# Expert tiles of two 64-row units, each with an expert of its own, in place of 128-row tiles of one expert

## The chip, the core and the metric

The kernel runs on one core of a Trainium2 chip. The metric is the device time of one execution in microseconds (us). The core has a matrix engine (TensorE: PE in the profile, its weight loads PEld), a vector engine (VectorE, DVE), a scalar engine (ScalarE, ACT), a general engine (GpSimd, POOL) and a queue engine for transfers (SyncE, SP). Each takes its instructions in order. They run beside each other and wait for each other through semaphores. Matrix products land in PSUM, eight banks of it; everything else stands in SBUF or in device memory.

## What is computed

The input is 8 sequences of 256 rows with 128 features, 2048 rows in all, in fp32. Six layers follow each other. Two of them, the first and the third, are a mixture of experts; between them stands a causal attention of 16 heads with 8 features each, and after them come a gated mixer, a layer of nine gated shifts, and the mixer again.

```python
x = x + 0.5 * moe(layernorm(x))      # L0_ffn
x = x + attention(layernorm(x))      # L0_attn
x = x + 0.5 * moe(layernorm(x))      # L0_ffn
x = x + 0.5 * mixer(layernorm(x))    # L1_ffn
x = x + shifts(layernorm(x))         # L1_attn
x = x + 0.5 * mixer(layernorm(x))    # L1_ffn
```

The layer that the change is about, cut to its core. Each row goes to 2 of 8 experts, so there are 4096 pairs of a row and an expert:

```python
normed = rmsnorm(x, norm_weight)
probs = softmax(normed @ router_weight.T)
topk_w, topk_idx = top_k(probs, 2); topk_w = topk_w / sum(topk_w)
for e in range(8):
    gate, up = split(normed @ gate_up_weight[e].T)    # 352 columns each
    out_e = (silu(gate) * up) @ down_weight[e].T      # 352 to 128
    moe_out += combine[:, e] * out_e
return x + alpha * moe_out
```

## The kernel before

**A planner writes the order.** No loop issues instructions directly. The kernel records operations with their engine, an estimated duration, what they need, and the buffers that they take and free (`Work`, `Op`, `Buf`). `Work.issue` then goes through the ready operations, takes the one that can start first by its own estimates (nearly equal starts go to the one with the longest way to the end), and emits it. This fixes the order on every engine. Constants called `BIAS` move whole groups of operations ahead or back in that ranking. When the planner foresees an idle matrix engine, it fills the time with matmuls of no use (`pw`), which keep that engine's clock up. All instructions pass one helper, so nearly every row of the profile bears its line, L65; rows are told apart by their tiles. The row of value loads bears L74.

**Groups.** The rows stand in four groups of 512 (`NG`, `GT`), each of four 128-row blocks.

**The expert layer.** `moe_route` norms a group, writes it to device memory (`rows0`, `rows1`), multiplies by the router weights and finds the two best experts of each row. `moe_plan` runs twice in a layer: after the first two groups (`whole` false), and after all four. It counts rows by expert and gives each pair a slot such that every 128-row tile holds one expert. Then it inverts this: `hits` marks which tile a pair is in, `is_at` marks which row of the tile it has, times the row's number, and `find` multiplies both on the matrix engine, which gives for every tile the list of rows to gather (`take`). `which_expert` and `side_by_side` give each tile its expert (`expert`). `ASIDE` names the blocks of `is_at` that ScalarE makes; VectorE makes the rest.

Since an expert's last tile may be part empty, `TILES` is 39 for 32 full tiles, 9 of which come from the first plan. `moe_experts` gathers the rows of a tile (`xs`, one indirect transfer by GpSimd), transposes them (`pt`) and scales them by the norm weight (`nT`). `moe_tile` does the rest: a value load brings the tile's expert number into a register of the matrix engine (`number`), which then addresses the weights (`gu`, `dw`, resident in SBUF); two products of 352 columns (`pg`, `pu`); SiLU on ScalarE (`sg`); the product with `pu` on VectorE (`hid`); three transposes (`ph`), a copy out of PSUM on ScalarE (`hT`), three accumulating products (`po`), a copy on VectorE (`ys`), and a store to device memory by SP. Beginning a tile waits for tiles two and three behind it, so that about three tiles are under way at once. `moe_back` scales the group's own rows on ScalarE (`own_rows`), gathers both results of each row (`back`), and adds them with their weights.

**Attention.** Scores (`sc`) run on strips of 32 rows of the matrix array, weighted values (`po<-ep,va`) on strips of 32 columns, four strips at once. Masks, transposes and projections use the full array. The last tiles of the first expert layer run among the first groups' attention, and the second expert layer starts where the attention ends.

Of the kernel before, what the change touches and what calls it, by code (L numbers as in the profile page):

```python
# [19 lines left out]
P = 128  # L20
NG = 4
GT = 4
# [8 lines left out]
TILES = 2 * NT + 7  # L31
# [4 lines left out]
BIAS = (10.0, 28.0, 18.0, 0.0, 19.0, 22.0, -6.0)  # L36
# [14 lines left out]
ASIDE = ((1,), (2, 5))  # L51
FOLD = ((4, 4, 1), (2, 2, 2, 2, 1), (4, 4, 1), (4, 2, 1, 1, 1))


class InOrder:
# [16 lines left out]
    def value_load(self, *args, **kw):  # L72
        with self.tc.issue_after(self.last.ins):
            return self.engine.value_load(*args, **kw)  # L74

# [18 lines left out]
class Op:  # L94
    def __init__(self, engine, us, do, needs, takes, uses, lag, spare):
        self.engine, self.us, self.do, self.lag, self.spare = engine, us, do, lag, spare
        self.takes, self.uses = takes, uses
        self.needs = [n for n in needs if n is not None]
        self.out, self.end, self.rank, self.back = None, None, None, 0.0


class Work:
# [25 lines left out]

    def __getattr__(self, name):
        if name not in ("pe", "dve", "act", "pool", "sp"):  # L130
            raise AttributeError(name)
        return lambda us, do, *needs, **kw: self.op(name, us, do, needs, **kw)

    def start(self, op):
        t = self.free.get(op.engine, 0.0)
# [84 lines left out]
def tile_macaron(ctx: ExitStack, tc: tile.TileContext, a: dict, out: bass.AP):  # L220
# [64 lines left out]
    with nc.allow_low_precision("zeros and ones"):  # L285
# [25 lines left out]
    minus_tok = ctile("minus_tok", [P, NT])  # L311
    nc.vector.tensor_scalar(minus_tok, tok1, -1.0, None, ALU.mult)
# [16 lines left out]
    va = [ctile(f"va{k}", [P, GT, NH, 32]) for k in range(2)]  # L329
# [9 lines left out]
            "t": 11, "q": 10, "p": 4, "mix": 2, "yTs": 2, "yTg": 2, "vT": 2,  # L339
# [15 lines left out]
    w.idle = idle  # L355

# [100 lines left out]

    def moe_layer(n, first):

        few = 2 * GT * first - 7  # L460
# [6 lines left out]
        for name, shape, dtype in (  # L467
            ("top", [P, NT, 8], F32), ("which", [P, NT, 8], U32), ("w", [P, NT, 2], F32),
            ("ab", [P, 2, NT], F32), ("rs", [P, NT], F32), ("slot", [P, 2 * NT], U32),
            ("take0", [P, few], U32), ("take1", [P, TILES - few], U32), ("expert", [1, TILES], I32),  # L470
# [12 lines left out]
    def moe_route(g, r):  # L483
# [33 lines left out]
        def scale_rows():  # L517
            nT = wtile(tag, "nT", (P, GT * P))
            nc.scalar.activation(
                nT, pt.out.rearrange("p t d -> p (t d)"), AF.Copy, scale=norm_w  # L520
            )
            return nT

        nT = w.act(0.69, scale_rows, pt, fewer, uses=[b1], takes=[nTb])
# [83 lines left out]
    def moe_plan(r, whole):  # L608
# [10 lines left out]
        def small(name, shape, dtype=F32):  # L619
# [4 lines left out]
                oh=2 * NT * E, m=NT * E, slot=NT * E, past=3 * NT * E, sums=P, hit=wide,  # L624
# [70 lines left out]
        def ends():  # L695

            whole = small("whole", [P, E])
            nc.vector.tensor_scalar(whole, placed.out[:, nt, :], -63.5, 1.0 / P, ALU.add, ALU.mult)
            nc.vector.tensor_scalar(whole, whole, ROUND, ROUND, ALU.add, ALU.subtract)
            nc.vector.tensor_tensor_scan(r["end"], one8, whole, 0.0, ALU.mult, ALU.add)  # L700
            nc.vector.tensor_scalar(r["full"][:, 0, :], whole, float(P), None, ALU.mult)
            nc.vector.scalar_tensor_tensor(
                r["base"], r["end"], float(P), r["full"][:, 0, :], ALU.mult, ALU.subtract
# [14 lines left out]
        def all_ends():  # L718
# [9 lines left out]
            nc.vector.tensor_scalar(left, left, 63.5, 1.0 / P, ALU.add, ALU.mult)  # L728
# [3 lines left out]
            if soon:  # L732
# [4 lines left out]
                    full[:, 2, :], nr[:, 1, :], float(P), full[:, 1, :], ALU.mult, ALU.add  # L737
# [5 lines left out]
            for k in range(parts):  # L743
# [9 lines left out]
                up[:, 0, :], at2[:, 0, :], float(P), r["both"], ALU.mult, ALU.subtract  # L753
            )
            nc.vector.tensor_tensor(up[:, 1:, :], at2[:, 1:, :], at2[:, :-1, :], ALU.subtract)
            nc.vector.tensor_scalar(up[:, 1, :], up[:, 1, :], -1.0, float(P), ALU.add, ALU.mult)
            if soon:
                nc.vector.tensor_tensor(up[:, 2, :], up[:, 2, :], nr[:, 1, :], ALU.subtract)
                nc.vector.tensor_scalar(up[:, 2, :], up[:, 2, :], float(P), None, ALU.mult)
# [13 lines left out]
        def prepare():  # L773
            full = r["full"]
            nc.vector.tensor_scalar(full[:, 1, :], full[:, 0, :], float(P), None, ALU.add)
# [38 lines left out]

        def find(k, at):
            if k == 0:
                v["pi"] = bank([P, ns], "pi")
            for j in range(GT):
                i = GT * k + j
                nc.tensor.matmul(  # L820
                    v["pi"], lhsT=at.out[:, j, :], rhs=v["hit"][:, i, :], start=(i == 0),
# [3 lines left out]
        def is_at(k):  # L825
            tag = "ata" if k in by_act else "at"
            at = wtile(tag, tag, (P, GT, P), F16)
            for j in range(GT):
                i = GT * k + j
                token = tok1[:, i % nt : i % nt + 1]  # L830
                if k in by_act:
# [4 lines left out]
                    nc.scalar.activation(  # L836
                        at[:, j, :], at[:, j, :], AF.Relu, bias=token,
                        scale=minus_tok[:, i % nt : i % nt + 1],
                    )
                else:  # L840
                    nc.vector.tensor_scalar(
                        at[:, j, :], iota_r, v["row"][:, i : i + 1], token, ALU.is_equal, ALU.mult
                    )
            return at

        found = None
        for k in range(2 * nt // GT):
            ab = Buf("ata" if k in by_act else "at")
            at = (w.act if k in by_act else w.dve)(
                2.0 if k in by_act else 0.68, lambda k=k: is_at(k), rowed, takes=[ab]  # L850
            )
            found = w.pe(
                0.3, lambda k=k, at=at: find(k, at), at, hit, found,
# [9 lines left out]
        def which_expert():  # L863
# [6 lines left out]
                le, until.rearrange("p k e -> p (k e)"), float(-n0), tok1[:, 0:1], ALU.add,  # L870
# [12 lines left out]
        def side_by_side():  # L883
            pe = bank([1, ns], "pe")
            nc.tensor.matmul(
                pe, lhsT=v["ef"][0:ns, :], rhs=ident[0:ns, 0:ns], start=True, stop=True
# [5 lines left out]
            0.17, lambda: nc.vector.tensor_copy(r["expert"][:, n0:n1], aside.out), aside,  # L892
# [9 lines left out]
    def moe_experts(r, sizes):  # L902
# [4 lines left out]
        for h in range(2):  # L907
            plan = r["plan"][h]
            rows = r["all_stored" if h else "stored"].values()
            for n in sizes[h]:  # L910
# [28 lines left out]
                def scale_rows(n=n, pt=pt):  # L939
                    nT = wtile("nT", "nT", (P, GT * P))  # L940
                    nc.scalar.activation(
                        nT[:, : n * P], pt.out.rearrange("p t d -> p (t d)")[:, : n * P], AF.Copy,
                        scale=norm_w,
# [3 lines left out]
                nT = w.act(0.2 + 0.125 * n, scale_rows, pt, uses=[b1], takes=[nb])  # L947
# [10 lines left out]
    def moe_tile(r, plan, k, nT, nb, j, pus, turned, downs, numbers):  # L958
# [3 lines left out]
        def number():  # L962
            numbers[k] = nc.tensor.value_load(
                r["expert"][0:1, k : k + 1], min_val=0, max_val=E - 1
            )

        known = w.pe(0.03, number, plan["experts"], *pus[-2:-1], lag=0.8)

        def product(c):
            wt = gu[:, bass.ds(numbers[k], 1), :].rearrange("p o h -> p (o h)")  # L970
            out = bank([P, HID], "pg" if c == 0 else "pu")
            nc.tensor.matmul(
                out, lhsT=nT.out[:, bass.ts(j, P)], rhs=wt[:, HID * c : HID * (c + 1)],
                start=True, stop=True,
            )
            return out

        pg = w.pe(0.6, lambda: product(0), known, nT, weights, *pus[-1:], *turned[-2:-1], *downs[-3:-2],
                  takes=[bg], uses=[nb], spare=3)
        pu = w.pe(0.6, lambda: product(1), pg, takes=[bu], uses=[nb])  # L980
# [34 lines left out]
        def keep():  # L1015
            hT = wtile("hT", "hT", (P, len(HC), P))
            nc.scalar.copy(hT, ph.out)
            return hT

        hT = w.act(0.48, keep, ph, takes=[tb], uses=[bh])  # L1020

        def down():
            po = bank([P, P], "po")
            wt = dw[:, bass.ds(numbers[k], 1), :, :].rearrange("p o c d -> p (o c) d")
            for c in range(len(HC)):
                nc.tensor.matmul(
                    po, lhsT=hT.out[:, c, :], rhs=wt[:, c, :], start=(c == 0),
                    stop=(c == len(HC) - 1),
                )
            return po  # L1030

        po = w.pe(0.67, down, hT, takes=[bo], uses=[tb])
        downs.append(po)

        def result():
            ys = wtile("ys", "ys", (P, P))
            nc.vector.tensor_copy(ys, po.out)
            return ys

        ys = w.dve(0.29, result, po, takes=[yb], uses=[bo])  # L1040
# [6 lines left out]
    def moe_back(g, r, stored):  # L1047
# [4 lines left out]
        if g < r["first"]:  # L1052
            until = 2 * GT * r["first"] + E
        elif r["soon"] and g < r["soon"]:
            until = 2 * GT * r["soon"] + E

        def own_rows():
            for t in range(GT):
                i = GT * g + t
                nc.scalar.activation(  # L1060
                    x[g][:, t, :], x[g][:, t, :], AF.Identity,
                    bias=r["ab"][:, 1, i : i + 1], scale=r["ab"][:, 0, i : i + 1],
                )

        changes(g, w.act(1.7, own_rows, hold["affined"], *tokens[g].given, *tokens[g].read))
# [37 lines left out]
    def attention():  # L1103
# [6 lines left out]
        def constants(mask, step):  # L1110
# [20 lines left out]
        va_free = [  # L1131
            [w.pool(1.4, lambda v=v: nc.gpsimd.memset(v[:, :, :, DK:32], 1.0))] for v in va
        ]
# [8 lines left out]
        def enter(g):  # L1142
# [6 lines left out]
            def keep(tag, name, src):  # L1149
                dst = wtile(tag, name, (P, GT * P))  # L1150
                nc.scalar.copy(dst, src)
                return dst

            yT = w.act(
                0.6, lambda: keep("nT", "yT", pt.out.rearrange("p t d -> p (t d)")), pt,
# [9 lines left out]
            cT = w.act(0.6, lambda: keep("cT", "cT", pc.out), pc, takes=[cb], uses=[b2])  # L1165
# [5 lines left out]
            for h2 in range(2):  # L1171
# [23 lines left out]
                def put(k, h2=h2, pj=pj):  # L1195
                    hg = 2 * h2 + k // 2
                    if k % 2 == 0:
                        nc.scalar.copy(box["qT"][:, hg, :], pj.out[k])
                    elif k == 1:
# [8 lines left out]
                for k in range(4):  # L1208
                    entered.append((w.dve if k == 1 else w.act)(
                        0.69 if k % 2 else 0.6, lambda k=k, f=put: f(k), pj, ones,  # L1210
# [4 lines left out]
            def value_rows():  # L1215
                pv = bank([P, GT * P], "pv")
                for t in range(GT):
# [7 lines left out]
            values = w.dve(  # L1225
                0.69,
                lambda: nc.vector.tensor_copy(
                    va[g % 2][:, :, :, 0:DK],
# [134 lines left out]
    def weighted(i, q, s, group, va_free):  # L1363

        g, t0 = i // 2, 2 * (i % 2)
        vb, ab, tb = Buf("b"), Buf("av"), Buf("b")

        def values():
            po = bank([P, 4, P], "po")
            for hg in range(4):  # L1370
                for k in range(q + 1):
                    for j in range(4):
                        nc.tensor.matmul(
                            po[32 * j : 32 * j + 32, hg, :],
                            lhsT=va[g % 2][:, t0 + k, 4 * hg + j, :],
# [11 lines left out]
        def keep():  # L1387
            av = wtile("av", "av", (P, 4, P))
            nc.scalar.copy(av, po.out)
            return av  # L1390

        av = w.act(0.6, keep, po, takes=[ab], uses=[vb])
# [26 lines left out]
        def keep_o():  # L1419
            oT = wtile("oT", "oT", (P, 2, P))  # L1420
            nc.scalar.copy(oT, pt.out[:, 0:2, :])
            return oT

        oT = w.act(0.4, keep_o, pt, takes=[ob], uses=[b1])
# [16 lines left out]
    def mix(g, n):  # L1441
# [8 lines left out]
        def keep():  # L1450
            yT = stile("yTs", "yTs", (P, 2, S + 1))
            nc.scalar.activation(yT[:, :, 0:1], one8[:, 0:2].unsqueeze(2), AF.Copy, scale=0.0)
            nc.scalar.copy(yT[:, :, 1 : S + 1], pt.out.rearrange("p (b t) d -> p b (t d)", b=2))
# [328 lines left out]
```

## Time and profile before

| | us |
|---|---|
| median of 3 runs | 516.03 |
| lowest and highest of them | 515.32, 517.52 |
| the profiled execution | 516.23 |
| its span, first to last instruction | 514.2 |

The profile lists the busy time of each engine, slices of the span, the chain of work that ended last (followed back from the end), and groups of instructions with their mean duration, shapes and what they waited for. A matmul in fp32 shows as two records, its two passes; a transpose shows as one. Matmuls overlap, so that a row's mean duration says less than the distance between two starts.

```profile
PE   7778889999999999999999999899999999999995
DVE  7866323436776897577768268634336537989960
ACT  3416537644436546546547563547645476666542
PEclk9989889999999999999999999799999999999998
```

These are 40 slices of 12.9 us each; a digit is the busy share in tenths, PEclk the granted clock in tenths. The expert layers lie in slices 3 to 12 and 24 to 32.

```profile
L65 PE MATMUL pg<-gu,nT 128*128 x156 | 62.4, 483 | 4.0 <-issue 1.9 <-ACT nT L65 1.6 <-DMA rows<-ep 0.5
L65 PE MATMUL po<-ep,va 128*32 128x128 f32 x768 | 24.3, 275 | 0.0
L65 ACT COPY hT<-ph 128x384 f32<-128x384 f32 x78 | 37.1, 478 | 55.5 <-PE ph L65 52.5 <-PE pu L65 2.4 <-PE po L65 0.4
L65 ACT ACTIVATE sg<-pg 128x352 f32<-128x352 f32 x78 | 36.2, 464 | 36.4 <-PE pg L65 34.7
L65 DVE TENSOR_TENSOR hid<-sg,pu 128x352 f32<-128x352 f32 x78 | 40.6, 521 | 68.7 <-PE pu L65 53.4 <-ACT sg L65 11.0 <-ACT nT L65 2.6
L65 DVE COPY ys<-po 128x128 f32<-128x128 f32 x78 | 22.2, 289 | 25.4 <-PE po L65 21.5 <-PE pt L65 1.6
```

A group's row reads: line, engine, operation, tile written and tiles read, the part of the matrix array (rows*columns), shapes, how often; then busy time in us and mean ns of one; then the engine's idle time just before, and what ended it.

### The profile page before, as it was taken

To read this page: it belongs to the slowest core of one execution; us is meant where nothing else is said; L and a number is where in the kernel's file an instruction comes from. 1 tells how busy PE (TensorE), PEld (TensorE's weight loads), DVE (VectorE), ACT (ScalarE), POOL (GpSimd) and SP (SyncE) were. 2 spreads that over 40 slices of the span, in tenths; PEclk is the share of its full clock that TensorE was granted. 3 is DMA by queue.
4 is the path that set the end of the run, shared out by engine and by line. 5 is a ranking of instruction groups with operands and counts; after the bars stand their busy time and mean duration, and the time that the engine had idled before them with its cause. 6 is when DMAs were issued, how large, how long until landed. Compare 5 with 4: busy or idle time off the path is not lost.

```text
span 514.2 us, 12524 instructions
## 1 busy us (share of the span) xinstructions
PE 485.9 (94%) x4594; PEld 344.7 (67%) x4594; DVE 321.1 (62%) x1119; ACT 272.5 (53%) x584; POOL 225.4 (44%) x237
## 2 busy tenths in 40 slices
PE   7778889999999999999999999899999999999995
PEld 3435767877676666777777776577887875575673
DVE  7866323436776897577768268634336537989960
ACT  3416537644436546546547563547645476666542
POOL 8060578456203720000000340478657758867631
PEclk9989889999999999999999999799999999999998
DMA  8850122223101100000100020122332210000001
GB/s 270 262 164 23 49 71 57 61 62 70 27 17 33 54 18 3 23 3 3 64 3 3 23 68 11 41 84 57 71 67 72 66 38 20 2 1 1 22 20 41
DMA packets 27034, 26.24 MB, mean 51 GB/s; under 512 B 4064, under 2 KB 24288, under 8 KB 26560
## 3 DMA queue, kind: packets, MB, share of 16 engines
q1 hardware_dynamic: 21232, 15.60, 9.9%
q0 software_dynamic: 4544, 9.32, 7.5%
q8 instruction: 38, 0.62, 0.5%
q10 hardware_dynamic: 1200, 0.53, 0.4%
q14 instruction: 20, 0.16, 0.1%
HBM read 17.18 MB, written 9.31 MB: 51 GB/s over the span
## 4 chain that ended last, share of the span: by engine, by line
PE 69%; DVE 13%; POOL 5%; issue 4%; DMA 4%; ACT 4%; POOLq 0%; SPq 0%; DVEq 0%; ACTq 0%
PE sc L65 17%; PE po L65 15%; PE pg L65 8%; PE pu L65 8%; PE ph L65 5%; PE pt L65 4%; DVE x L65 3%; PE pgt L65 2%; POOL back L65 2%; PE pr L65 2%; DMA rest<-in_rest 2%; DMA rows<-n 2%; DVE p L65 2%; PE pv L65 2%; PE pj L65 1%
## 5 line engine op out<-in xcount | busy, mean ns | idle before, releaser
L65 POOL DMA_INDIRECT xs<-rows,take x78 | 74.6, 956 | 120.8 <-DVE take L65 42.8
L65 POOL DMA_INDIRECT back<-ys,slot x64 | 61.4, 959 | 61.5 <-DMA ys<-ys 33.7
L65 DVE TENSOR_TENSOR hid<-sg,pu 128x352 f32<-128x352 f32 x78 | 40.6, 521 | 68.7 <-PE pu L65 53.4
L65 ACT ACTIVATE ep<-sc 128x512 f32<-128x512 f32 x96 | 52.0, 595 | 52.6 <-PE sc L65 52.6
L65 PEld LDWEIGHTS po<-dw,hT 128*128 128x128 f32 x468 | 62.8, 192 | 15.4 <-ACT hT L65 2.0
L65 PE MATMUL po<-dw,hT 128*128 x468 | 65.5, 277 | 1.2 <-ACT hT L65 0.4
L65 ACT COPY hT<-ph 128x384 f32<-128x384 f32 x78 | 37.1, 478 | 55.5 <-PE ph L65 52.5
L65 PE MATMUL pg<-gu,nT 128*128 x156 | 62.4, 483 | 4.0 <-issue 1.9
L65 POOL TENSOR_TENSOR stats<-stats,minus_half 128x4 f32<-128x4 f32 x28 | 28.7, 1025 | 82.5 <-DVE stats L65 81.9
L65 PE MATMUL pu<-gu,nT 128*128 x156 | 60.6, 470 | 0.0
L65 PEld LDWEIGHTS sc<-kT,qT 32*128 32x128 f32 x768 | 46.0, 186 | 19.6 <-issue 16.8
L65 PE MATMUL sc<-qT,kT 32*128 32x128 f32 x768 | 56.2, 283 | 0.7 <-DVE qT L65 0.5
L65 ACT ACTIVATE sg<-pg 128x352 f32<-128x352 f32 x78 | 36.2, 464 | 36.4 <-PE pg L65 34.7
L65 PE MATMUL sc<-kT,qT 32*128 32x128 f32 x768 | 55.1, 283 | 0.0
L65 DVE TENSOR_REDUCE mtmp<-sc 128x4 f32<-128x512 f32 x64 | 41.3, 684 | 15.5 <-PE sc L65 15.5
L65 PEld LDWEIGHTS sc<-qT,kT 32*128 32x128 f32 x768 | 46.9, 186 | 3.3 <-issue 2.1
L65 PE MATMUL ph<-ident,hid 128*128 128x128 f32 x234 | 39.6, 282 | 1.8 <-DVE hid L65 1.7
L65 PEld LDWEIGHTS ph<-ident,hid 128*128 128x128 f32 x234 | 30.3, 146 | 16.3 <-issue 8.3
L65 PE MATMUL pw<-before,ones_b 128*128 128x512 bf16 x125 | 36.0, 426 | 3.3 <-POOL ones_b L65 2.4
L65 DVE COPY ys<-po 128x128 f32<-128x128 f32 x78 | 22.2, 289 | 25.4 <-PE po L65 21.5
L65 PE MATMUL pgt<-yTg,rest 128*128 128x512 f32 x72 | 34.2, 595 | 0.7 <-DVE p L65 0.7
L65 PEld LDWEIGHTS pu<-gu,nT 128*128 128x128 f32 x156 | 27.2, 198 | 7.7 <-issue 1.0
(204 smaller groups left out, 885.7 us busy)
## 6 DMA issues: line engine op xcount, KB each, us to landing
ys<-ys SPq DMA_DIRECT2D x78, 64.0 KB, 2.0
gu<-in_guT SPq DMA_DIRECT2D x2, 1408.0 KB
rest<-in_rest SPq DMA_DIRECT2D x1, 1280.0 KB, 9.8
xs<-rows,take POOLq DMA_INDIRECT x78, 2.5
x<-in_x SPq DMA_DIRECT2D x4, 256.0 KB, 4.1
dw<-in_dwT SPq DMA_DIRECT2D x1, 1024.0 KB
rows<-rows SPq DMA_DIRECT2D x2, 512.0 KB, 4.7
back<-ys,slot POOLq DMA_INDIRECT x64, 2.5
```

Source lines behind the costliest of these rows:

```text
L65: ins = do(*args, **kw)
```

## The change

A tile still holds 128 rows, but they are two units of 64, and each unit has its own expert. Slots are counted in units (`U` = 64): there are 64 full ones and at most 7 more, so 36 tiles (`TILES`) in place of 39, and 12 of them in the first plan in place of 9. `which_expert` now gives two numbers a tile.

In `moe_tile` each product becomes two, one for each unit, which write rows 0 to 63 and 64 to 127 of the same bank; each uses 64 columns of the array. The first takes its weights from `gu` or `dw` through the matrix engine's register, as before. The second takes them from a copy: for every tile, its second expert's weights are copied to a fixed place (`wg`, 704 columns; `wd`, 384 columns; three buffers each) by ScalarE or VectorE, which load the number into a register of their own first (`Engines` gets `number` for this).

The planner may now choose the engine of some operations (`either`): the weight copies, `nT`, `hT`, `ys`, `own_rows` and several copies of the attention, mixer and shift layers go to ScalarE or VectorE, whichever ends them first by its estimates. `BIAS` and `ASIDE` have other values.

In `moe_plan`, `is_at` gives ones and zeros; the row's number is multiplied in on the other side (`values`, on GpSimd, between `hits` and `find`). `moe_back` waits for 20 tiles in place of 24 for the first two groups. The buffer `va` of the attention is packed more tightly, and `mix_weights` moves behind the second plan.

```diff
-TILES = 2 * NT + 7
+U = 64
+TILES = (4 * NT + 7 + 1) // 2
-BIAS = (10.0, 28.0, 18.0, 0.0, 19.0, 22.0, -6.0)
+BIAS = (27.0, 38.0, 18.0, 10.0, 25.0, 29.0, 1.0)
-ASIDE = ((1,), (2, 5))
+ASIDE = ((3,), ())
+LEAN = {"act": 0.0, "dve": 0.15}
...
+    def number(self, at):
+        with self.tc.issue_after(self.last.ins):
+            _, values = self.tc.nc.values_load_multi_w_load_instructions(
+                at, [self.engine.engine], min_val=0, max_val=E - 1,
...
+    def either(self, act, dve, do, *needs, **kw):
+        op = self.op("act", min(act, dve), None, needs, **kw)
+        op.choice = {"act": act, "dve": dve}
+        op.do = lambda: do(op.engine)
+        return op
...
     def start(self, op):
+        if op.choice is None:
+            return self.start_on(op)
+        best = None
+        for engine, us in op.choice.items():
+            op.engine = engine
+            t = self.start_on(op)
...
+            us += LEAN.get(engine, 0.0)
+            if best is None or t + us < best[0]:
+                best = (t + us, t, engine)
+        op.engine, op.us = best[2], op.choice[best[2]]
+        return best[1]
...
-        few = 2 * GT * first - 7
+        few = (4 * GT * first - 7) // 2
...
+        def values():
+            val = small("val", wide, F16)
+            for c in range(2):
+                cs = slice(nt * c, nt * c + nt)
+                nc.gpsimd.tensor_tensor(
+                    val[:, cs, :], v["hit"][:, cs, :],
+                    tok_h[:, 0:nt].unsqueeze(2).to_broadcast([P, nt, ns]), ALU.mult,
+                )
+
+        valued = w.pool(0.3 + 0.002 * 2 * nt * ns, values, hit)
...
                     nc.vector.tensor_scalar(
-                        at[:, j, :], iota_r, v["row"][:, i : i + 1], token, ALU.is_equal, ALU.mult
+                        at[:, j, :], iota_r, v["row"][:, i : i + 1], None, ALU.is_equal
                     )
...
+        def copied(engine, tag, src, width):
+            e = {"act": nc.scalar, "dve": nc.vector}[engine].number(
+                r["expert"][0:1, 2 * k + 1 : 2 * k + 2]
+            )
+            dst = wtile(tag, tag, (P, width))
+            src = src[:, bass.ds(e, 1)].rearrange("p o h -> p (o h)")
+            copies(engine, dst, src)
+            return dst
+
+        gb, db = Buf("wg"), Buf("wd")
+        gates = w.either(
+            1.15, 1.05, lambda e: copied(e, "wg", gu, 2 * HID), plan["experts"], weights,
+            *pus[-3:-2], takes=[gb],
+        )
+        backs = w.either(
+            0.85, 0.76, lambda e: copied(e, "wd", dw.rearrange("p e c d -> p e (c d)"), len(HC) * P),
+            plan["experts"], weights, *pus[-3:-2], takes=[db],
+        )
...
-            nc.tensor.matmul(
-                out, lhsT=nT.out[:, bass.ts(j, P)], rhs=wt[:, HID * c : HID * (c + 1)],
-                start=True, stop=True,
-            )
+            for h in range(2):
+                rows = slice(U * h, U * h + U)
+                wt = gates.out
+                if h == 0:
+                    wt = gu[:, bass.ds(numbers[k], 1), :].rearrange("p o h -> p (o h)")
+                nc.tensor.matmul(
+                    out[rows, :], lhsT=nT.out[:, j * P + U * h : j * P + U * h + U],
+                    rhs=wt[:, HID * c : HID * (c + 1)], start=True, stop=True,
+                )
...
             for c in range(len(HC)):
-                nc.tensor.matmul(
-                    po, lhsT=hT.out[:, c, :], rhs=wt[:, c, :], start=(c == 0),
-                    stop=(c == len(HC) - 1),
-                )
+                for h in range(2):
+                    rows = slice(U * h, U * h + U)
+                    wt = backs.out[:, c * P : c * P + P]
+                    if h == 0:
+                        wt = dw[:, bass.ds(numbers[k], 1), c, :].rearrange("p o d -> p (o d)")
+                    nc.tensor.matmul(
+                        po[rows, :], lhsT=hT.out[:, c, rows], rhs=wt, start=(c == 0),
+                        stop=(c == len(HC) - 1),
+                    )
```

## The prediction, made before the changed kernel ran

> **What bounds the kernel now.** I read the page first: busy times, then the chain of work that ended last.
>
> ```profile
> PE 485.9 (94%) x4594; PEld 344.7 (67%) x4594; DVE 321.1 (62%) x1119; ACT 272.5 (53%) x584; POOL 225.4 (44%) x237
> ...
> PE 69%; DVE 13%; POOL 5%; issue 4%; DMA 4%; ACT 4%; POOLq 0%; SPq 0%; DVEq 0%; ACTq 0%
> ```
>
> The matrix engine is busy nearly always, and 69% of the chain lies on it. Next the table of stages, for two stretches of the second expert layer, and the chain in the second of them:
>
> ```profile
> 308.00:327.00 19.00, 17.30 (x112) 10.57 (x111) 16.90 (x81) 9.39 (x23) 0.00 (x0) 0.92 0.03 8
> ...
> 366.00:379.00 13.00, 13.00 (x81) 10.37 (x80) 4.40 (x12) 6.19 (x13) 5.46 (x7) 1.00 0.40 56
> ```
> ```profile
> 366.07 0.44 PE pt L65 x4
> 366.51 0.59 PE pg L65 x2
> 367.10 0.67 PE po L65 x6
> 367.77 0.59 PE pu L65 x2
> 368.37 0.33 PE ph L65 x3
> ```
>
> Columns of the first: stretch, length, busy time of PE, PEld, DVE, ACT and POOL, clock, DMA. From 366 to 379 us PE is full, and the chain holds nothing but PE: a tile costs 0.59 + 0.59 + 0.33 + 0.67 + a quarter of 0.44 = **2.29 us**, weight loads hidden. DVE and ACT have half their time free or more. The other stretch differs: the plan runs there on DVE, and PE has run out of tiles, as the timeline shows (start, duration, what):
>
> ```profile
> 67.51 1.30 PE L65 MATMUL pg<-gu,nT 128*128 x2 [1.94 <-issue]
> ...
> 316.28 5.13 PE L65 MATMUL pw<-before,ones_b 128*128 128x512 bf16 x23
> ...
> 327.12 0.87 PE L65 MATMUL ph<-ident,hid 128*128 128x128 f32 x3
> ```
>
> From 316.28 to 327.12 there are 10.8 us of fillers and of plan products, while the chain is on DVE; in the first layer PE waits 1.94 us for the tenth tile.
>
> **Part 1: six tiles fewer.** 6 × 2.29 = **-13.7 us** of PE. Do two strips of 64 columns run side by side? Before has no such pair, but the weighted values use four strips of 32:
>
> ```profile
> 173.30 0.28 PE L65 MATMUL sc<-qT,kT 32*128 32x128 f32 x2
> 173.50 1.95 PE L65 MATMUL po<-ep,va 128*32 128x128 f32 x64
> 175.39 0.60 PE L65 MATMUL sc<-mask_k,ident_b 128*128 128x512 bf16 x2
> 175.93 0.38 PE L65 MATMUL sc<-kT,qT 32*128 32x128 f32 x2
> ...
> 179.41 1.08 PE L65 MATMUL po<-ep,va 128*32 128x128 f32 x32
> 180.42 0.60 PE L65 MATMUL sc<-mask_q,ident_b 128*128 128x512 bf16 x2
> ```
>
> 64 passes take 175.39 - 173.50 = 1.89 us, 32 take 1.01, so a pass of 128 columns costs 0.0275 us, a quarter of the 0.67 / 6 = 0.11 on the full array. Four strips share the array fully; I take the same for two. The products of a tile then keep their price.
>
> **Part 2: changing the array's shape.** The same rows show what strips cost. The 32 passes are worth 0.88, so 0.13 us is spent in a group's start and on leaving the shape. Entering: two mask passes of 512 columns take 0.43 (a chain piece has four in 0.86), yet the scores start 0.54 after the masks, 0.11 later; and the values start 0.20 after the last scores, whose pass takes 0.11. So a round trip costs 0.09 to 0.11 plus 0.13, **0.22 us**. Before, no expert tile pays this. As built, the changed kernel goes from the full array to 64-column strips 84 times for its 72 tiles, since every `ph` and `pt` lies on the full array between `pg`, `pu` and `po`: 84 × 0.22 = **+18.5 us**. Some 16 of them lie where PE has time (the 12 tiles of the first layer's first plan, about 4 around the second layer's plan), -3.5. The row-strip scores with masks bound it above: 34 records take 1.64 in the chain, less 32 × 0.0275 and 0.43, leaves 0.33. I keep 0.22, from column strips. Here a rule speaks against the change: the Trainium skill, TensorEngine Tiling (Array Packing), gives up to twice the speed for 64 columns under Theoretical Speedup, but says under Key Properties that changing the mode, other than the tile, drains the engine. By the speedup alone the two parts give -13.7; by the row behind the drain they give -13.7 + 15.0 = **+1.3**. The tiling as such gains nothing.
>
> **Part 3: the gaps.** First layer: 12 tiles of the first plan in place of 9 are 6.9 us more work before the second plan is needed. That covers the 1.94 wait and the half clock behind it (67.51 to 70.95, three products some 1.15 apart in place of 0.59, 1.7 us), and the waits of plan products for ScalarE, 1.9 us near 52 to 53, go with `ASIDE`: -5.0 (between -1 and -8). Second layer: as built, DVE runs from the counts to the new expert numbers without one `hid` of a tile, so PE still starves. PE has 4.7 us of tile work after the counts there against 3.4; DVE makes 32 `at` in place of 24, each with one operation less. The chain has five of the old in 0.95, 0.19 each; between 0.10 and 0.19 I take 0.15, 4.8 us in all, about as before. -1.5 (between +2 and -5). `values` on POOL, 2 × 0.96 us by the 1284 ns of `q<-p` with 512 columns, runs while DVE makes the first two blocks of `at`: 0, or 0.5 without that cover.
>
> **Part 4: copies and loads.** As built, ACT takes 61 `wg` and 34 `wd`, DVE 11 and 38; each has a register load in front. Rows:
>
> ```profile
> L74 PEldq TENSOR_LOAD <-expert x78: 295/301/499, 25.0 to 403.2; - x78
> L65 ACT ACTIVATE ka<-rk 128x512 f32<-128x512 f32 x8 | 5.1, 633 | 0.2
> L65 DVE COPY va<-pv 128x512 f32<-128x512 f32 x4 | 2.8, 692 | 1.4 <-PE pv L65 0.8 <-PE po L65 0.6
> ```
>
> ACT reads 512 columns from SBUF in 0.63; at the slope between `hT` (384: 0.478) and `ep` (512: 0.595), 704 cost about 0.80 and 384 about 0.52. Per tile ACT then holds `sg` 0.46, `hT` 56/72 × 0.48, `ys` 24/72 × 0.36, `nT` 0.16, copies 0.68 + 0.25, loads 1.32 × 0.30: **2.44 us**. PE needs 2.29 + 1.17 × 0.22 = **2.55**. So ACT fits by a hair, and DVE (`hid` 0.52, copies, `ys`, `hT`: 1.5) more easily. A load on ACT isn't in the trace: below it costs nothing, hidden behind the instruction still running; above 0.45, with the 0.15 register step that follows PE's. I take PE's row. The Trainium skill, DMA: Bandwidth & Descriptors, Latency and other measured facts, gives some 600 ns as the floor of a tensor load; by that ACT had 2.84 and were the bound. The row is half of it and on this kernel, so I follow the row. For `sg` queued behind a 0.8 us copy, and `ph` behind `sg`, I add +1.0 (0 to +8): three tiles are under way, but ACT is at 96%.
>
> POOL loses 6 gathers of 0.94 us, SP 6 stores: hidden. `own_rows` and copies that change engine lie beside PE: 0. `moe_back` needing 20 tiles, not 24, meets full PE work: 0.
>
> **Sum:** -13.7 + 18.5 - 3.5 - 5.0 - 1.5 + 1.0 = **-4.2 us**. The profiled execution's span becomes 510.0 and its time, 2.0 more, 512.0. It stood at 516.23, the median at 516.03, so no correction.
>
> **Rivals.** *Shape changes at the row-strip price* (slower). Place: every `ph`. Price 0.33: 68 × 0.33 = 22.4 in place of 15.0, so 519.4. It decides from 0.28 us a round trip, where 68 of them eat 19.2. For it: the rule and the scores; against it: column strips at 0.22. *ACT becomes the bound* (slower): loads exposed at 0.55 make ACT 2.77 a tile, 0.22 over PE, on some 55 tiles in full stretches +12, 524. It decides from 0.44, where the gain is gone. For it: some 140 us of loads and copies added to two engines in the expert stages (ACT 61 × 0.80 + 34 × 0.52 + 95 × 0.30, DVE 11 × 0.89 + 38 × 0.56 + 49 × 0.30); against it: the load row. *The gaps close* (faster): cheap `at` and no waits in either plan, loads hidden behind running instructions: -5 in the second layer and -2 more in the first, 505. Against it: no `hid` within the second plan's DVE run. *The strips don't share*: each tile pays 1.84 more, 72 × 1.84, about 645; the values speak against it.
>
> **Chances.** My forecast, with its own range of 508 to 516: 0.46. Gaps close: 0.20. Row-strip price: 0.13. ACT the bound: 0.18. Strips in turn: 0.02. What a measurement can tell from no change is about 0.5%, 2.6 us. Faster: 0.32 of the forecast plus the 0.20. Same: the rest of the forecast and the mild ends of the slower rivals, 0.20. Slower: 0.28. The range that leaves out two in ten is 503 to 523.
>
> **What would show it.** Right: `pg` to `pu` still 0.59 apart; about 0.1 us between `ph` and the strips on either side; no wait between the first plan's tiles and the next in the first layer; PE full in the second layer's tiles, about 2.55 us each; ACT near 2.4 us a tile. Wrong: strip starts a pass apart; `sg` or `hid` ending PE's waits tile after tile; register loads over 0.44 us on ACT.

## The result, and the profile after

The changed kernel takes 511.79 us, median of 4 runs (510.68 to 512.99); the kernel before took 516.41 beside it. The ratio is **0.9905, 95% interval 0.988 to 0.9931**. In a later set of runs the same kernel stood at 511.28 against 517.35, ratio 0.9882 (0.9858 to 0.9906). The profiled execution took 510.68, 5.6 less than the one of before. The prediction said 512.0.

In two of the four sets of experiments, the disturbed ones below, the kernel before itself took 577 and 585 us, and the traces of those sets show ScalarE and VectorE standing for up to 13.8 us at a time, released by something that they cannot name, so that totals from there are compared with nothing outside their set, and the stretches read there are those in which the matrix engine (PE) is full.

From the page of the changed kernel: busy times, the shares of the chain that ended last, and the slices of PE and of its granted clock.

```profile
PE 485.4 (95%) x5206; PEld 312.9 (62%) x5206; DVE 351.0 (69%) x1217; ACT 293.4 (58%) x580; POOL 224.9 (44%) x240
PE 74%; DVE 11%; POOL 4%; issue 3%; ACT 1%; DMA 0%; POOLq 0%; ACTq 0%; DVEq 0%
PE   7978999999999999999999999599999998999995
PEclk9899999999999999999999999689999999999998
```

PE's busy time has not moved (485.9 before, 485.4 now), though 6 tiles of work are gone and the fillers in it fell from 36.0 us to 28.7. Something has filled the place of those 13.7 us. The clock's two slices of 8 in the first layer's tiles, the fifth and sixth, are gone (the third before and the second now lie ahead of the first tile); the second layer has 6 and 8 where it had one 7.

The chain of work in the second layer's tiles shows what filled it (start, duration, what). In the kernel before, `pg`, `pu`, `po` and `ph` took 0.59, 0.59, 0.67 and 0.33 here.

```profile
362.03 0.66 PE po L70 x12
362.69 0.48 PE ph L70 x3
363.16 0.74 PE pg L70 x4
363.90 0.48 PE ph L70 x3
364.38 0.74 PE pu L70 x4
365.12 0.66 PE po L70 x12
365.78 0.59 PE pg L70 x4
```

The chain holds nothing but PE, as before. A `pg` or `po` that follows another product in strips costs what it did. But every `ph` costs 0.15 more, and so does the product behind it. That is 0.30 for one round trip from strips to the full array and back.

The table of stretches, for the second layer's plan, the time behind it, and a full stretch (columns: stretch, length, busy time of PE, PEld, DVE, ACT and POOL, clock, DMA share, GB/s):

```profile
312.00:329.00 17.00, 11.41 (x98) 7.01 (x97) 15.23 (x71) 6.19 (x15) 1.63 (x2) 0.77 0.07 20
329.00:346.00 17.00, 16.80 (x134) 10.19 (x135) 6.54 (x22) 9.98 (x19) 12.61 (x14) 0.83 0.25 67
346.00:384.00 38.00, 38.00 (x357) 23.28 (x355) 23.80 (x73) 26.50 (x46) 27.08 (x25) 1.00 0.26 61
```

Around the plan PE stands, where before it ran fillers, and the granted clock is a half from 321.0 to 334.7; before it was a half from 323.8 to 330.6. In the full stretch PE has no idle time, and DVE and ACT are busy 23.8 and 26.5 us of 38, their register loads not counted.

The difference by stage, from starts of `pg` and of the last matmul in both traces. Each stage but the last holds the same number of tiles in both kernels. Round trips are changes from the full array to strips in the trace; the last column uses the prediction's 0.22 for each where it put them on the path, and leaves out its +1.0 for ACT, which it gave to no stage.

| stage | before | after | difference | round trips | by the prediction's terms |
|---|---|---|---|---|---|
| start to the 12th tile of the first layer | 72.0 | 64.4 | -7.6 | 13 | -5.0 |
| to the last tile ahead of the gap at the second layer's plan (33 tiles) | 242.3 | 251.8 | +9.5 | 40 | +8.8 |
| to the first tile of that plan (4 tiles) | 22.3 | 25.6 | +3.3 | 5 | -1.5 |
| to the last matmul (30 tiles before, 24 after) | 171.4 | 160.8 | -10.7 | 26 | -8.0 |

Differences are of the unrounded times. One execution is not exact to the us: the trace of the control c1, the same kernel once more, has 66.0, 253.8, 25.2 and 160.4 in these rows.

### The profile page after: what moved, and what is told of

Its sections match the earlier page's. It is cut to its first block, busy times and chain, and to the rows that moved or that the text cites. A ratio compares the mean times of both kernels' runs of the same rounds, so it can differ in the third digit from the quotient of the medians.

```text
span 508.5 us, 13883 instructions
## 1 busy us (share of the span) xinstructions
PE 485.4 (95%) x5206; PEld 312.9 (62%) x5206; DVE 351.0 (69%) x1217; ACT 293.4 (58%) x580; POOL 224.9 (44%) x240
## 4 chain that ended last, share of the span: by engine, by line
PE 74%; DVE 11%; POOL 4%; issue 3%; ACT 1%; DMA 0%; POOLq 0%; ACTq 0%; DVEq 0%
PE sc L70 18%; PE po L70 15%; PE pg L70 9%; PE pu L70 9%; PE ph L70 6%; PE pt L70 5%; PE pgt L70 2%; DVE at L70 2%; PE pv L70 2%; POOL q L70 2%; PE pr L70 2%; PE pj L70 2%; POOL back L70 2%; DVE x L70 1%; PE pk L70 1%
## 5 line engine op out<-in xcount | busy, mean ns | idle before, releaser
L70 PEld LDWEIGHTS po<-dw,hT 128*64 128x64 f32 x432 | 49.9, 138 | 19.7 <-issue 15.9
L70 PE MATMUL po<-dw,hT 128*64 x432 | 60.0, 277 | 0.9 <-ACT sg L70 0.3
L70 PE MATMUL po<-wd,hT 128*64 128x128 f32 x432 | 60.1, 277 | 0.0
L70 ACT COPY wg<-gu 128x704 f32 x61 | 47.4, 779 | 19.7 <-PE pu L70 9.8
L70 PE MATMUL pg<-gu,nT 128*64 x144 | 57.4, 480 | 0.6 <-ACT nT L70 0.5
L70 PE MATMUL pg<-wg,nT 128*64 128x352 f32 x144 | 57.4, 480 | 0.0
L70 PE MATMUL pu<-wg,nT 128*64 128x352 f32 x144 | 56.2, 472 | 0.0
L70 PE MATMUL pu<-gu,nT 128*64 x144 | 56.2, 472 | 0.0
L70 PEld LDWEIGHTS po<-wd,hT 128*64 128x64 f32 x432 | 49.9, 138 | 0.0
L70 ACT ACTIVATE sg<-pg 128x352 f32<-128x352 f32 x72 | 33.4, 463 | 27.6 <-PE pg L70 22.3
L70 ACT COPY hT<-ph 128x384 f32<-128x384 f32 x56 | 26.7, 479 | 29.1 <-PE ph L70 27.5
## 6 DMA issues: line engine op xcount, KB each, us to landing
rows<-rows SPq DMA_DIRECT2D x2, 512.0 KB
```

Of the source, the lines that this page charges most:

```text
L70: ins = do(*args, **kw)
```

## Experiments

My theory behind the runs: PE sets the end; the six tiles are a clean gain; changing the array's shape takes most of it back. Rivals: ScalarE with its copies and loads is the bound; the changes of shape are hidden.

### e1: strips alone, in the kernel before

```diff
-            nc.tensor.matmul(out, lhsT=nT.out[:, bass.ts(j, P)], rhs=wt[...], ...)
+            for h in range(2):
+                rows = slice(64 * h, 64 * h + 64)
+                if h == 1:
+                    wt = gu[:, k % E, :]
+                nc.tensor.matmul(out[rows, :], lhsT=nT.out[:, j * P + 64 * h : ...], rhs=wt[...], ...)
```

`po` is split in the same way.

> The kernel before, still 39 tiles a layer of 128 rows and without weight copies, but each gate, up and down product goes in two 64-column strips. The second strip reads the weights of a fixed expert (tile number modulo 8), so the choice of its expert is left out. Nothing else changes, so this is the price of changing the array's shape alone. My theory: about 91 round trips (78 tiles at 1.17) of two changes at 95 ns measured in the changed kernel, 17 us, less some 3 where PE waits anyway: 530, between 528 and 532. Rival, the change of shape hides behind the weight loads: 516, within 2. Rival, the row-strip price of 0.33 a round trip: 541 or more.

Measured: 610.63 against 577.24, ratio 1.0589 (1.0535 to 1.0643), in a disturbed set, so the total doesn't decide. A full stretch does. Four tiles with one `pt`, from `pg` to `pg`, take 437.93 to 448.27, **10.34 us, with 4 round trips**; in the kernel before the same four take 366.51 to 375.68, 9.17. Per round trip that is 0.29, without any copy or choice of engine. The chains at both ends of the two stretches, e1 and then before:

```profile
437.93 0.74 PE pg L65 x4
448.27 0.73 PE pg L65 x3
```
```profile
366.51 0.59 PE pg L65 x2
375.68 0.59 PE pg L65 x2
```

The rival that the change of shape hides has fallen.

### e2, e2b, e3: without copies, without loads

```diff
-                wt = gates.out
+                wt = gu[:, k % E, :]                  # e2: no copy, no load (dw likewise)
...
-            src = src[:, bass.ds(e, 1)].rearrange("p o h -> p (o h)")
+            src = src[:, k % E]                       # e3: copy without the load
```

> The changed kernel without any weight copy and without the register loads in front of them: the second strip reads the weights of a fixed expert (tile number modulo 8) where they lie, so the choice of the second unit's expert is left out. My theory, PE sets the end and the copies lie beside it: 510 to 512. Rival, ACT is the bound or nearly (copies and loads make sg late): 505 or less.

> The changed kernel with its 144 weight copies, but without the register loads in front of them on ACT and DVE: each copies a fixed expert (tile number modulo 8), so the choice of the second unit's expert is left out. My theory, loads of 0.28 to 0.30 lie beside PE: 511 to 512. Rival, loads hold up the sg and hid behind them: 507 or less, and then most of what taking the copies away gives.

> The changed kernel without weight copies and register loads again (a fixed expert, tile number modulo 8, for the second strip, so the choice of the second unit's expert is left out), beside a kernel before that is not held up by DMA. A tile in full stretches took 2.59 us without them and 2.60 with them in the first try. My theory: 509 to 512, the copies lie beside PE. Rival, the loads and copies cost 5 or more: 506 or less.

Measured, all in disturbed sets: e2 1.0068 (1.0046 to 1.0091), e3 1.0151 (1.0093 to 1.0209), e2b 1.0073 (1.005 to 1.0097). None of these totals answers its question, since the changed kernel did not run beside them. What stopped the engines there looks like this (timeline of e3; in brackets the idle time before and its releaser). That it is DMA, as some expectations say, no trace shows:

```profile
395.54 0.51 ACT L70 COPY wd<-dw 128x384 f32<-128x384 f32 x1 [6.57 <-remote]
395.54 0.29 DVE L70 COPY ys<-po 128x128 f32<-128x128 f32 x1 [8.62 <-remote]
```

The full stretches do answer, where kernels with the same number of round trips are set side by side (four tiles with one `pt` each; times from the chains of work):

| kernel | copies | loads | round trips | four tiles, us |
|---|---|---|---|---|
| before | - | - | 0 | 9.17 |
| changed | yes | yes | 4 | 10.30 |
| changed | yes | yes | 5 | 10.61 |
| e2 | no | no | 4 | 10.31 |
| e2 | no | no | 5 | 10.61 |
| e2b | no | no | 4 | 10.30 |
| e3 | yes | no | 5 | 10.61 |

The ends of three of them, for the changed kernel, e2 and e3:

```profile
358.23 0.74 PE pg L70 x4
368.53 0.74 PE pg L70 x4
```
```profile
417.30 0.74 PE pg L70 x4
427.61 0.74 PE pg L70 x4
```
```profile
409.25 0.74 PE pg L70 x4
419.86 0.74 PE pg L70 x3
```

With or without copies, four trips are 10.30; the fifth trip adds 0.30. So in full stretches copies and loads cost PE nothing, and ACT is not the bound. Outside full stretches this stays open, for the totals point both ways: side by side, e3 with its copies took 4.6 us more than e2 without, but e10 below, without copies, 7.6 more than e9 with them.

### e4: the old engines

```diff
+    def either(self, act, dve, do, *needs, only=None, **kw):
...
+        op.choice = {"act": act, "dve": dve} if only is None else {only: ...}
```

> The changed kernel with every operation that existed before on the engine that it had before; only the weight copies may still choose. My theory, the free choice gives little, since PE is the bound and DVE takes more of the copies instead: 512 to 515. Rival, the choice is what pays for the change (ACT overloaded without it, sg late tile after tile): 519 or more.

Measured: 1.0192 (1.0127 to 1.0257), in the same disturbed set as e3, whose interval overlaps. In full stretches the choice of engine is worth at most 0.1 us in four tiles: with five trips they take 10.60 (407.29 to 417.89), as in the table, and with four 10.39 (417.89 to 428.28). What it is worth in the total stays open.

### c1 and e5: control, and 39 tiles

```diff
-TILES = (4 * NT + 7 + 1) // 2
+TILES = 2 * NT + 7
```

> The changed kernel itself, as the control for what runs beside it. My theory: the gain of 0.95% belongs to the kernel, ratio 0.988 to 0.993. Rival: the gain belongs to chips on which stores and gathers land quickly; where all kernels wait for DMA now and then (the first four experiments ran beside a kernel before of 577 us), the ratio is 1.00 to 1.02.

> The changed kernel with 39 tiles a layer in place of 36, the three last ones of each layer empty. My theory: a tile is worth 2.6 us of full PE (read from pg to pg in the second layer), so 6 tiles cost 14 to 17 more than the control. Rival, the number of tiles matters little because gaps absorb them: 8 or less.

Measured: c1 0.9882 (0.9858 to 0.9906), so the gain was seen twice. Whether there is a gain in a disturbed set, as the rival asks, was not tried with the changed kernel itself; its near relatives e2, e3 and e4 were slower than the kernel before there.

e5: 532.09, ratio 1.028 (1.0258 to 1.0303), **20.8 more than the control**, above my 14 to 17. Six tiles at 2.29 are 13.7, and 12 more round trips (96 in place of 84 as built) at 0.30 are 3.6. The last 3.5 lies in the second layer, where three tiles cost some 13 us; no single wait explains it. The rival, that gaps absorb the tiles, has fallen.

### e6 and e7: the second layer's plan

```diff
+    w.back = 10.0                                     # e6
     moe_plan(r1, True)
...
-                        at[:, j, :], iota_r, v["row"][:, i : i + 1], None, ALU.is_equal
+                        at[:, j, :], iota_r, v["row"][:, i : i + 1], token, ALU.is_equal, ALU.mult   # e7
```

> The changed kernel with a lower priority for the operations of the second layer's second plan, so that five hid of tiles under way are placed between them on DVE, where the changed kernel has one. My theory: PE starved there for 11 us because DVE makes no hid; with them three more tiles run in the gap and the half clock behind it goes: 3 to 5 below the control. Rival, the plan ends later by what the tiles gain, or the tiles are the same work moved: within 1.5 of the control.

> The changed kernel with the token number multiplied again in the comparison that makes the blocks at, as before, and without the step values on POOL. My theory: DVE beside POOL is what made the first eight at cost 0.31 each; the eight lose 1.2, the other 24 gain about 0.03 each, so within 1 of the control. Rival, the wait for POOL sets the plan's end: 2 or more below the control.

e6: 512.52, ratio 0.9905 (0.9885 to 0.9925), 1.2 above the control. **My theory fell.** PE's timeline in e6:

```profile
336.99 6.00 PE L70 MATMUL pw<-before,ones_b 128*128 128x512 bf16 x27
```

The tiles did move into the plan. But the plan's last `pi` then came 48.9 us after the layer's first `pg`, in place of 43.3 in the control, and PE ran out of tiles behind it: 27 fillers. The 13th tile, the first of the second plan, came at 58.5 after that `pg`, in place of 56.1. So the gap is not made by the order on DVE alone. As I read it, what sets it is the way from the counts over DVE's run, the list and the gathers to the 13th tile, with only the first plan's 12 tiles to fill it. The 1.2 itself is within the noise, and the new order also makes three round trips more (87), 0.9 us by the price above.

e7 (`values` on POOL goes with this edit): 513.40, ratio 0.9917 (0.9893 to 0.9942), 2.1 above the control; intervals overlap. With the row's number in the comparison 32 `at` take 7.24, 0.226 each. In the changed kernel (timeline of DVE, then of POOL):

```profile
321.09 2.59 DVE L70 TENSOR_SCALAR at<-iota_r,row 128x128 f16<-128x128 f16 x8
324.53 3.98 DVE L70 TENSOR_SCALAR at<-iota_r,row 128x128 f16<-128x128 f16 x24
```
```profile
321.35 1.63 POOL L70 TENSOR_TENSOR val<-hit,tok_h 128x384 f16<-128x384 f16 x2 [18.74 <-DVE at L70]
```

24 of them cost 0.166 each; the first eight cost 0.32. Two single records hold all of the excess: the `at` that start right behind the two `val` last 0.825 and 0.865, as long as `val` itself (0.845 and 0.826), where their neighbours follow each other at 0.163. So `values` is not free: 1.2 us of DVE. It still takes less than the fused form, 6.57 against 7.24. The rival of e7, a faster kernel, fell.

### e9 and e10: turning in strips too

```diff
-                nc.tensor.transpose(ph[:, c, :], hid.out[:, c0 : c0 + P], ident)
+                turned_in_strips(ph[:, c, :], hid.out[:, c0 : c0 + P])
...
+    def turned_in_strips(dst, src):
+        for h in range(2):
+            rows = slice(U * h, U * h + U)
+            nc.tensor.matmul(dst[rows, :], lhsT=src[:, rows], rhs=ident, start=True, stop=True)
```

The expert tiles' `pt` is turned likewise. e10 is e9 with e2's edit.

> The changed kernel with the turns of hid (ph) and of the gathered rows (pt of the expert tiles) made in two 64-column strips as well, as products with the identity, so that the array keeps its shape from tile to tile; the order of the instructions stays, and 104 of 309 changes of shape go. My theory: each costs 0.096 us of full PE, 10.0 in all, of which some 2 lie where PE waits: 7 to 9 below the changed kernel, about 503. Rival, ACT is the bound next (2.4 us a tile against 2.35 of PE then): 4 or less below it. Rival, the changes of shape lie beside something else and cost nothing: within 1 of it.

> The same with ph and pt in strips, and without weight copies and their register loads: the second strip reads the weights of a fixed expert (tile number modulo 8), so the choice of the second unit's expert is left out. My theory, PE stays the bound: within 2 of the kernel with the copies. Rival, ACT is the bound there: 4 or more below it.

Measured, in a disturbed set: e9 1.0491 (1.0434 to 1.0549), e10 1.0603 (1.0546 to 1.066). In a full stretch of e9 the chain reads:

```profile
443.50 0.66 PE ph L70 x12
444.15 0.59 PE pg L70 x4
449.14 0.87 PE pt L70 x16
```

The 0.15 on either side is gone, as the theory wants. But `ph` is now 12 records, not 3, and takes 0.66: a product in fp32 makes two passes, where the transpose made one, and `pt` doubles too. Four tiles take 10.84 (439.17 to 450.01), more than the changed kernel's 10.30; the pieces agree: 4 × (0.59 + 0.66 + 0.59 + 0.66) + 0.87 = 10.87. e10 takes 10.85 (438.25 to 449.10), so the copies cost nothing in this stretch either; why its total is 7.6 above e9's, and not within 2, is not traced. I had left the second pass out of my expectation.

### e12: a planner that knows the shape

```diff
+            late = {op: t + (0.5 if self.turned(op) else 0.0) for t, op in starts}
+            t, op = min(starts, key=lambda s: (late[s[1]], -s[1].rank))
...
+            op.end = t + op.us + (0.15 if self.turned(op) else 0.0)
...
-        pg = w.pe(..., *turned[-2:-1], *downs[-3:-2], takes=[bg], uses=[nb], spare=3)
+        pg = w.pe(..., *turned[-3:-2], *downs[-4:-3], takes=[bg], uses=[nb], spare=2)
```

`turned(op)` is true for a PE step whose shape differs from the last one's; `pg`, `pu` and `po` are marked as strips. `BIAS` is (29, 36, 18, 14, 17, 25, -5).

> The changed kernel with a planner that knows of the array's shape: a step of the matrix engine in another shape than the one before is put back by 0.5 us and costs 0.15, a pg may start one tile earlier, and the seven weights of the order are set anew for it. The work is the same; the round trips from the full array to 64-column strips fall from 84 to 40. My theory, a round trip costs 0.30 us (0.096 out, 0.096 back, and some 0.055 more for the first pass in each shape): 44 of them are 13 us, of which some 2 to 4 lie where PE waits, so 9 to 11 below the changed kernel, a ratio to the kernel before of about 0.968 to 0.972. Rival, the price of the prediction (0.22): 6 to 8 below. Rival, hid and hT come late when tiles go in pairs (or ACT is the bound): 3 below or less, or slower. If the kernel before is held up by DMA here (570 or more), full stretches of the second layer decide: 2.45 us a tile or less by the theory, 2.60 by the last rival.

Measured, beside a kernel before of 517.56: **505.10, ratio 0.9763 (0.9731 to 0.9794)**. This beats both kernels, and lies 6.2 below the control of the other undisturbed set. The chain now runs through tiles in pairs:

```profile
351.89 0.66 PE po L70 x12
352.54 0.59 PE pu L70 x4
353.13 0.81 PE ph L70 x6
353.94 0.74 PE pg L70 x4
354.68 0.66 PE po L70 x12
```

One `ph` of six transposes serves two tiles (2 × 0.33 + 0.15). Four tiles take 9.70 (349.31 to 359.01) with 2 round trips; 10.30 with 4: again **0.30 each**. On the price the theory is right and the rival at 0.22 wrong. On the total it is not: 9 to 11 were expected, and 6.2 came, which is what the rival gave. The traces place the rest. From the full array to 64-column strips e12 goes 41 times in place of 84. From the second layer's first `pg` to the last matmul e12 takes 204.4 us, the control 216.5: 12.1 less. But from the first layer's first `pg` to there it takes 258.7, the control 255.2, with 11.7 us of idle time and fillers on PE in place of 6.5. So the new order gave back in the first layer and the attention a part of what it saved. The traced execution of e12, 501.59, lies 3.5 below its median, so these sizes are rough.

## Why the prediction was right, and where it was wrong

The total was right in part by luck, since terms cancelled: the round trips cost 5.4 us more than forecast, and waits and fillers that the sum had left in place, in part not traced, gave that back.

**Part 1, six tiles fewer, -13.7:** right. Tiles without a round trip still cost what they did, e5 shows it from the other side, and the two strips do share the array: their records start 7 ns apart, and `pg` of both takes 0.59.

**Part 2, the round trip at 0.22: the term that was mis-sized. It costs 0.30.** Three comparisons give 0.29 to 0.30: e1 against before, five trips against four, e12 against the changed kernel. (The changed kernel against before, 10.30 and 9.17, gives 0.28, as a `po` in strips is 0.01 shorter.) I read 0.09 to 0.11 for entering and 0.13 for a group's start and leaving. The trace of the changed kernel gives 0.096 for each change, both ways, and some 0.055 more for the first pass in the new shape, again both ways: 2 × 0.151. The longer first pass of the full array on return was in neither of my readings, since I took the 0.13 from the spacing of groups. The 68 trips that I put on the path then cost 20.4 in place of 15.0, and the tiling as such loses 6.7, not 1.3. The row-strip row, 0.33, which I kept as the upper end, was the nearer one; that rival had nearly the right price and the wrong outcome, because other work and gaps took off more than it allowed. The Trainium skill's rule in TensorEngine Tiling (Array Packing), Key Properties, that a change of mode drains the engine, fits these traces, where each change costs time; the drain itself is not seen in them, and the price is the runs' own.

**Part 3, the first layer, -5.0:** the mechanism right, the size low. From the first `pg` to the 12th tile it takes 32.3 us in place of 39.0, 6.8 less, and that includes 13 round trips; the rest of the 7.6 lies ahead of the first tile. PE's idle time falls from 7.7 us (32.0 to 67.5) to 1.7 (32.0 to 65.0), and the half clock there is gone. (The control has a half clock from 33.8 to 37.2 and takes 32.3 too.) The term was taken from one wait, its half clock and three plan products, and left out smaller waits.

**Part 3, the second layer, -1.5: wrong in sign.** The same four tiles took 3.3 longer, five round trips included. The price of `at` was too low: 32 took 6.57, not 4.8, and 1.2 of that comes from `values`, taken as free (two `at` stood 0.6 us each). This used up what more tiles were to cover, but it is not where the 3.3 lies. From the start of the last `po` ahead of the gap to the first `ph` behind it PE takes 11.7 us before (315.44 to 327.12) and 11.8 now (317.38 to 329.19):

```profile
317.38 0.27 PE L70 MATMUL po<-dw,hT 128*64 x1
322.24 0.26 PE L70 MATMUL pi<-val,at 128*128 128x24 f16 x3 [4.04 <-DVE at L70]
329.19 0.87 PE L70 MATMUL ph<-ident,hid 128*128 128x128 f32 x3 [0.42 <-DVE take L70]
```

The difference lies behind that `ph`, where PE is full up to the 13th tile: 12.5 us in place of 9.4. Two `po` more stand there, 1.3, which the kernel before makes in the last stage, so this is no loss. Three and a half round trips are 1.0; the prediction had put them where PE has time. The rest, 0.7, goes with the clock, which the prediction left out: without fillers PE stands in the gap, and the half clock reaches 5.5 us into these tiles (to 334.7) in place of 3.5 (to 330.6). In e6, with tiles in the gap, the half clock lasts 6.8 us and not 13.65. That DVE runs without a `hid` in the plan was seen rightly, but e6 shows that placing some there does not close the gap.

**Part 4, ACT, +1.0:** nothing of it shows in full stretches (10.30 with copies, 10.31 without). The load is cheaper on ACT than the row of PE that I used:

```profile
L84 ACTq TENSOR_LOAD <-expert x95: 272/276/555, 26.1 to 403.7; - x95
```

The three times are the shortest, the median and the longest. The median is 276 ns, and the 704-column copy took 0.779 where I had 0.80. From 346 to 384 ACT is busy 26.5 us and issues 19 copies, so 19 loads, 5.2: 31.7 in 14.8 tiles of 2.575, **2.15 a tile, not 2.44**. The Trainium skill's floor of some 600 ns for a tensor load (DMA: Bandwidth & Descriptors, Latency and other measured facts) made ACT the bound in the prediction's sum, 2.84 a tile; at 276 on this engine the measurement decides, and the row of the trace was the better guide.

**The last stage** gained 10.7, where six tiles and 26 trips at 0.30 give 5.9. Of the rest, 2.0 are nine fillers fewer (20 in place of 29, at 5.13 / 23), and 1.3 the two `po` that the kernel before still owed there; 1.5 is not traced. In the second stage 40 trips would be 12.0; 9.5 came in this trace and 11.6 in the control's, so two executions of one kernel differ by nearly as much as is missing.

## What to carry to other kernels

Splitting the array has a price beside the products: count how often the instruction order leaves the shape and comes back, price one round trip from the spacing of records on both sides of it, and put like shapes next to each other before splitting further. When a gap closes, ask what path sets the start of the work behind it; moving work into a gap gains nothing if the same path then makes a gap later. Compare kernels by full stretches of equal work when the totals are disturbed.

## What the runs showed of the hardware that I had not expected

- A change of the array's shape costs the same in the changed kernel's trace, medians of 94 to 98 ns, whether from or to 64-column, 32-column or 32-row strips. The first fp32 pass after it, some 55 ns longer, comes on top.
- Turning a block by a product with the identity takes twice the passes of a transpose in fp32: 0.66 against 0.33 for three blocks.
- Two DVE comparisons in f16, else 0.163 us apart, lasted as long as the POOL products that ran beside them: 0.825 and 0.865 us against 0.845 and 0.826.
